# A three-layer graph attention kernel: partly filled gather columns packed densely, moved by one-hot products

## The chip, the cores and the metric

The kernel runs on one core of a Trainium2 chip. Its time is the device time of one execution in microseconds (us), from the first to the last instruction. Five engines work side by side, each on its own stream of instructions: PE (matrix products; PEld loads its weights), DVE (vector work), ACT (scalar work, exponentials and scaled copies), POOL (here mostly the issuer of indirect DMAs, which gather rows by index) and SP (the issuer of plain DMAs). "Span" is the profiler's first to last instruction.

## What is computed

There are 6250 nodes with 256 features and 100000 edges sorted by their target. Two GATv2 layers (4 heads of 64) with a self loop, a residual and a layer norm are followed by one GAT layer (8 heads of 32), a residual and a layer norm.

```python
def _gatv2_layer(x, src, dst, n, Wl, Wr, att, b):
    xl = (x @ Wl).reshape(n, H, C)
    xr = (x @ Wr).reshape(n, H, C)
    e = jax.nn.leaky_relu(xl[src] + xr[dst], NEG_SLOPE)
    logits = jnp.einsum('ehc,hc->eh', e, att)
    m = jax.ops.segment_max(logits, dst, num_segments=n)
    ex = jnp.exp(logits - m[dst])
    denom = jax.ops.segment_sum(ex, dst, num_segments=n)
    alpha = ex / (denom[dst] + 1e-16)
    msg = xl[src] * alpha[:, :, None]
    out = jax.ops.segment_sum(msg, dst, num_segments=n)
    return out.reshape(n, H * C) + b
...
h = _gatv2_layer(x, src, dst, n, Wl1, Wr1, att1, b1)
h = jax.nn.elu(h)
h = _gatv2_layer(h, src, dst, n, Wl2, Wr2, att2, b2)
...
x = _layernorm(x + _L0_gnn_ref(...), axis=-1)
x = _layernorm(x + _L1_gnn_ref(x, W, a, src, dst), axis=-1)
```

The third layer's logits are `leaky_relu(s1[src] + s2[dst])`, with one number for each node and head, and its messages are rows `Wh[src]`.

## The kernel before

**Blocks and columns.** `make_plan` sorts the nodes by their number of incoming edges, the largest first, and cuts them into 49 blocks of 128 nodes, one node in each partition. A block's edges become columns: column j of block b holds, for each of its 128 nodes, the row of that node's j-th source, or a row "nobody" (number NP) with a logit of -1.5e38 where the node has fewer. `columns` computes from the edge count alone, with bounds of 3.5 standard deviations, how many columns each block needs: 27 in block 0 (the few edges beyond are moved by one-hot products, `find_few`, `few_logits`, `few_sum`), then 25, 24, 23, 22, 21, ... down to 9 in block 48, 803 in all. One column is one indirect DMA on POOL (`gather_rows`, L1438).

**Packs.** The last column of some blocks is needed by a part of the nodes only. Before, ten such columns share three gathers ("packs": blocks 3, 13, 17, 36; blocks 26, 40, 47, 48; blocks 31, 43), with fixed row counts. `pick_rows` copies their indices together by SP's DMAs, `gather_pack` gathers them, `lay_rows` copies each part into its column, and `lack_rows` fills the column's other partitions with "nobody". The plan checks that no node needs more (`most`, L996).

**Buffers.** `rows` holds nine tiles of up to nine columns; a block of layer 1 or 2 takes three (two from block 18 on, where columns and self row are 18 or fewer). A tile is free again when PE has added its columns up, or in layer 3 when DVE has weighted them.

**The order, written out by hand.** Every engine runs its instructions in the order of the code. In `layer2`, which serves layers 1 and 2, the main loop does for block b:

1. `attend(b)`: on DVE, logits by three passes over each chunk (L1797, L1800, L1801; the first chunk's first pass, `first_z`, L1777, was already done in the block before), then the maximum (L1579); on ACT the exponentials (L1587), in layer 1 a copy of source numbers into `spots`; then the table rows of block b-2 are copied and written by SP (L1917), and `first_z(b+1)`.
2. `finish(b-1)` on ACT, then `weighted_sum(b)`: DVE multiplies rows by weights (L1633), ACT does it for the last `few` columns (L1629, four heads each), PE adds all columns up (L1640).
3. `fetch(b+2)` issues the lists of block b+4 (L1887), the pack work and `gather(b+2)`; then `turns` transposes on PE (L1558) and makes the next tables.

In layer 2 `fetch(b+2)` moves ahead, into `attend(b)`, where the buffers allow. `find_few` runs before `gather(0)`, `turns(0)`, `fetch(1)` and `turns(1)` in layer 1. `sort_sources` orders the first three blocks' sources, so that the following layer can gather their first 14, 12 and 11 columns (`EARLY`) before the last four blocks' rows are written: `begin`, called after the last `gather` of a layer, with the table cut at the rows of the first 45 blocks. In layer 3 the loop is `gather(b+1)`, `attend(b)` (L2010), weighting and adding on DVE (L1662, L1674), and a scatter of the finished rows on POOL (L2040).

**The plan's end.** `make_plan` writes the list of each node to DRAM (`near_d`, L1237) in two halves. Between them stand seven gathers into `spare` (L1254), a tile that nothing reads.

The two lines that the change's last part touches:

```python
few = min(S // 3, cut[-1][1] - cut[-1][0] - 1) if i == 0 else (2 * S - 2) // 3
few = few if b + 1 < NB else 0
```

Of the kernel before, what the change touches and what calls it, by code (L numbers as in the profile page):

```python
# [47 lines left out]
def columns(E, N, NB):  # L48
# [30 lines left out]
    part = {}  # L79
    for b in range(len(EARLY), NB):  # L80
        c = cols[b] - 1
        n = max(8, -(-int(math.ceil(over[c] + 3.5 * sd[c] - P * b)) // 8) * 8)
        if n < P:
            part[b] = n
    packs, taken = [], set()
    for b in sorted(part):
        if b in taken or part[b] > P * 3 // 4:
            continue
        pack, at = [], 0
        for k in range(b, NB):  # L90
            if k in part and k not in taken and at + part[k] <= P:
                pack.append((k, at, part[k]))
                at += part[k]
        if len(pack) > 1:
            packs.append(pack)
            taken.update(k for k, _, _ in pack)
    return cols, low, high, held, packs
# [569 lines left out]
def kernel(  # L667
# [22 lines left out]
    cols, low, high, held, packs = columns(E, N, NB)  # L690
# [7 lines left out]
    node_i = plan.tile([P, NB], I32, name="node_i")  # L698
    fits = plan.tile([P, 1], I32, name="fits")
# [11 lines left out]
    with tc.manual_schedule():  # L711
        make_plan(
            tc, x, src, dst, ((wl1, wr1, att1), (wl2, wr2, att2)), (b1, b2), w3, a3,
            cols, low, high, held, packs, node_i, fits, ident, eps, nobody, att, wc, wh, fixed, xl1_d,
            near_d,
        )
        nc.vector.memset(done, 0)
# [4 lines left out]
    with tc.If(ok != 0):  # L722
        with tc.manual_schedule():
            tile_by_degree(
                tc, x, att1, b1, b2, w3, a3, out, [held] + cols[1:], packs, node_i, near_d, ident, eps, nobody,
                xl1_d, att, wc, wh, fixed, done,
            )
# [8 lines left out]
def make_plan(  # L736
    ctx, tc, x, src, dst, layers, biases, w3, a3, cols, low, high, held, packs, node_i, fits, ident, eps,
    nobody, att, wc, wh, fixed, xl1_d, near_d,
# [36 lines left out]
    SPARE = 7  # L775
# [218 lines left out]
    for pack in packs:  # L994
        for b, _, n in pack:
            nc.gpsimd.tensor_scalar(  # L996
                most[:, b : b + 1], part_of, float(n), float(cols[b] - 1), op0=OP.is_lt, op1=OP.add
            )
# [252 lines left out]
    spare = one.tile([P, SPARE, LONG], I32, name="spare")  # L1251
    left(1, nc.gpsimd)
    for k in range(SPARE):
        nc.gpsimd.indirect_dma_start(  # L1254
            out=spare[:, k, :], out_offset=None, in_=listed,
            in_offset=bass.IndirectOffsetOnAxis(ap=begin_i[:, k : k + 1], axis=1),
        )
# [12 lines left out]
    counts = one.tile([P, NB], F32, name="counts")  # L1270
# [26 lines left out]
def tile_by_degree(  # L1297
    ctx, tc, x, att1, b1, b2, w3, a3, out, cols, packs, node_i, near_d, ident, eps, nobody,
    xl1_d, att, wc, wh, fixed, done,
# [52 lines left out]
    late = consts.tile([P, len(EARLY)], F32, name="late")  # L1352
# [41 lines left out]
    packed = {b: (q, r, n) for q, pack in enumerate(packs) for b, r, n in pack}  # L1394
    opens = {pack[0][0]: q for q, pack in enumerate(packs)}
    shuts = {pack[-1][0]: q for q, pack in enumerate(packs)}
    picks = [consts.tile([P, len(packs)], I32, name=f"pick{k}") for k in range(2)]
    for pick in picks:
        nc.gpsimd.memset(pick, NP)
    held_rows = {}  # L1400

    def pick_rows(q, pick, of):

        for b, r, n in packs[q]:
            nc.sync.dma_start(pick[r : r + n, q : q + 1], of[:n, b, cols[b] - 1 : cols[b]])

    def gather_pack(b, pool, name, pick, table, width):
        q = opens[b]
        held_rows[q] = pool.tile([P, RW], F32, name=name)
        nc.gpsimd.indirect_dma_start(  # L1410
            out=held_rows[q][:, :width], out_offset=None, in_=table,
            in_offset=bass.IndirectOffsetOnAxis(ap=pick[:, q : q + 1], axis=0),
        )

    def lay_rows(b, rows, width):

        q, r, n = packed[b]
        nc.sync.dma_start(rows[-1][:n, rows_at[b], :width], held_rows[q][r : r + n, :width])

    rows_at = {}  # L1420

    def lack_rows(b, rows, cut, table, width):

        n = packed[b][2]
        rows_at[b] = cut[-1][1] - cut[-1][0] - 1
        nc.sync.dma_start(
            rows[-1][n:, rows_at[b], :width],
            bass.AP(tensor=table.tensor, offset=table.offset + NP * width, ap=[[0, P - n], [1, width]]),
        )

    def gather_rows(b, rows, cut, own, table, of, width, j0, j1):


        for g, (s0, s1) in zip(rows, cut):
            for j in range(max(s0 - own, j0), min(s1 - own, j1)):
                if j + 1 == cols[b] and b in packed:
                    continue
# [88 lines left out]
    def sort_sources(work, ps, b):  # L1526

        n = cols[b]
# [19 lines left out]
        if b + 1 == len(EARLY):  # L1548
            pb = ps.tile([P, b + 1], F32, name="pb", tag="tp")
# [148 lines left out]
    def layer2(i, table, of, width, start, own, finish, follow):  # L1698
# [5 lines left out]
        with ExitStack() as es:  # L1704
# [5 lines left out]
            packp = es.enter_context(tc.tile_pool(name=f"pack{i}", bufs=len(packs)))  # L1710
# [5 lines left out]
            def gather(b):  # L1716
                first = EARLY[b] if b in begun else 0
                rows, cut = begun.pop(b) if first else row_tiles(b, 1)
                if b in opens:
                    gather_pack(b, packp, "pack", picks[i], table, width)  # L1720
# [119 lines left out]
            if i == 0:  # L1840
                find_few(work, pst)
# [274 lines left out]
```

## Time and profile before

| what | value |
|---|---|
| median of 14 runs | 3236.54 us (3235.97 to 3238.51) |
| profiled execution | 3237.21 us |
| its span | 3235.4 us |
| POOL | 2412.9 us busy (75%), 2587 instructions |
| DVE | 2714.9 us busy (84%), 2609 instructions |
| PE | 1399.1 us busy (43%) |
| ACT | 1281.8 us busy (40%) |
| DMA | 397.64 MB, 123 GB/s |

From the issue times of POOL, the first row gather of layer 1 starts at 104.2 us; the early gathers of layer 2 at 1159.55 and the rest of its block 0 at 1206.2; those of layer 3 at 2157.95 and 2204.2; the last gather at 3215.6. DMA-issuing instructions of POOL count as busy here, those of SP don't. "Idle before" in a group is the time the engine stood still just ahead of it; "issue" means that nothing the profile shows was waited for.

### The profile page before, as it was taken

To read this page: it belongs to the slowest core of one execution; us is meant where nothing else is said; L and a number is where in the kernel's file an instruction comes from. 1 tells how busy PE (TensorE), PEld (TensorE's weight loads), DVE (VectorE), ACT (ScalarE), POOL (GpSimd) and SP (SyncE) were. 2 spreads that over 40 slices of the span, in tenths; PEclk is the share of its full clock that TensorE was granted. 3 is DMA by queue.
4 is the path that set the end of the run, shared out by engine and by line. 5 is a ranking of instruction groups with operands and counts; after the bars stand their busy time and mean duration, and the time that the engine had idled before them with its cause. 6 is when DMAs were issued, how large, how long until landed. Compare 5 with 4: busy or idle time off the path is not lost.

```text
span 3235.4 us, 25460 instructions
## 1 busy us (share of the span) xinstructions
PE 1399.1 (43%) x5424; PEld 1122.3 (35%) x5424; DVE 2714.9 (84%) x2609; ACT 1281.8 (40%) x5161; POOL 2412.9 (75%) x2587
## 2 busy tenths in 40 slices
PE   8266656666677754666566566770000000000000
PEld 6255545554565643545445455550000000000000
DVE  8599999898899978999989999994966767666677
ACT  3234444444445535777667777770000000000001
POOL 5677777777777777777777777777777777777776
PEclk9677887878888986887877888885555555555555
DMA  9544444444444454444444444544334433434343
GB/s 259 125 113 125 119 118 123 118 122 124 124 123 127 125 147 112 124 122 129 128 123 127 130 133 133 136 128 113 109 107 109 110 108 107 109 109 110 109 110 95
DMA packets 176463, 397.64 MB, mean 123 GB/s; under 512 B 50923, under 2 KB 93955, under 8 KB 176283
## 3 DMA queue, kind: packets, MB, share of 16 engines
q0 software_dynamic: 120608, 336.86, 39.8%
q1 hardware_dynamic: 53992, 57.08, 5.9%
q10 hardware_dynamic: 1700, 1.97, 0.3%
q8 instruction: 48, 0.79, 0.1%
q14 instruction: 115, 0.94, 0.1%
HBM read 354.60 MB, written 40.42 MB: 122 GB/s over the span
## 4 chain that ended last, share of the span: by engine, by line
POOL 25%; DVE 17%; issue 14%; DMA 5%; PE 4%; ACT 1%; DVEq 0%; POOLq 0%; SPq 0%; ACTq 0%
POOL g L1438 24%; DVE z L1800 3%; DVE lg L1801 3%; PE acc L1640 3%; DMA g<-xl_d,near_r 2%; DVE z L1797 2%; DVE z L1777 2%; DVE g L1633 2%; DMA g<-whs_d,near_r 2%; DVE weighted L1662 1%; POOL out L2040 1%; DMA out<-y,node_i 1%; DVE acc_v L1674 0%; DVE stats L1684 0%; ACT g L1629 0%
## 5 line engine op out<-in xcount | busy, mean ns | idle before, releaser
L1438 POOL DMA_INDIRECT g<-xl_d,near_r x1549 | 1465.7, 946 | 473.8 <-issue 419.1
L1640 PE MATMUL acc<-g,ident 128*128 128x256 f32 x3408 | 966.8, 452 | 631.0 <-DVE g L1633 316.6
L1640 PEld LDWEIGHTS acc<-g,ident 128*128 128x128 f32 x3408 | 777.5, 232 | 821.2 <-DVE g L1633 334.6
L1438 POOL DMA_INDIRECT g<-whs_d,near_r x756 | 717.7, 949 | 230.3 <-issue 220.2
L1629 ACT ACTIVATE g<-g,by 128x64 f32<-128x64 f32 x3080 | 744.9, 336 | 28.3 <-DVE by L1596 28.0
L1801 DVE TENSOR_REDUCE lg<-z 128x28 f32<-128x1820 f32 (+4 forms) x234 | 497.4, 2125 | 8.1
L1800 DVE TENSOR_TENSOR z<-z,at 128x1820 f32<-128x1820 f32 (+4 forms) x234 | 496.8, 2123 | 4.7
L1797 DVE TENSOR_TENSOR z<-g,pr 128x1820 f32<-128x1820 f32 (+3 forms) x138 | 299.7, 2172 | 44.5 <-DMA g<-xl_d,near_r 34.6
L1604 ACT ACTIVATE wt<-lg 128x128 f32<-128x128 f32 (+17 forms) x49 | 14.0, 285 | 799.8 <-DVE lg L1603 799.8
L1674 DVE TENSOR_REDUCE acc_v<-weighted 128x256 f32<-128x3584 f32 (+10 forms) x47 | 319.0, 6787 | 1.6
L1633 DVE TENSOR_TENSOR g<-g,at 128x256 f32<-128x256 f32 (+8 forms) x185 | 273.6, 1496 | 3.3
L1587 ACT ACTIVATE at<-lg,top 128x19 f32<-128x19 f32 (+14 forms) x392 | 115.3, 294 | 379.6 <-DVE top L1579 362.9
L1777 DVE TENSOR_TENSOR z<-g,pr 128x2080 f32<-128x2080 f32 (+4 forms) x96 | 197.9, 2062 | 72.5 <-DMA g<-xl_d,near_r 31.0
L2010 DVE TENSOR_TENSOR lg<-g,s_r 128x56 f32<-128x56 f32 (+4 forms) x111 | 23.0, 215 | 253.7 <-DMA g<-whs_d,near_r 232.2
L1662 DVE TENSOR_TENSOR weighted<-g,wt 128x1792 f32<-128x1792 f32 (+4 forms) x111 | 227.1, 2058 | 0.3
L1563 ACT COPY xT<-pt 128x256 f32<-128x256 f32 x147 | 50.2, 374 | 402.0 <-PE pt L1558 402.0
L1568 PE MATMUL pm<-wcat,xT 128*128 128x260 f32 x392 | 94.2, 383 | 1.4 <-ACT xT L1563 1.4
L1568 PEld LDWEIGHTS pm<-wcat,xT 128*128 128x128 f32 x392 | 74.2, 190 | 13.4 <-ACT xT L1563 2.1
L1587 ACT ACTIVATION_READ_ACCUMULATOR at<-lg,top 128x1 f32 x392 | 73.2, 187 | 0.0
L1568 PE MATMUL pm<-wh_cat,xT 128*128 128x272 f32 x196 | 58.0, 419 | 22.6 <-ACT xT L1563 22.6
L2040 POOL DMA_INDIRECT out<-y,node_i x49 | 49.8, 1017 | 23.0 <-issue 14.2
L1688 ACT ACTIVATE sd<-mv,eps 128x1 f32<-128x1 f32 x98 | 29.0, 296 | 93.0 <-DVE mv L1686 93.0
(267 smaller groups left out, 1592.6 us busy)
## 6 DMA issues: line engine op xcount, KB each, us to landing
g<-xl_d,near_r POOLq DMA_INDIRECT x1549, 2.8
g<-whs_d,near_r POOLq DMA_INDIRECT x756, 2.8
whs_d<-row SPq DMA_DIRECT2D x49, 132.0 KB
xl_d<-row SPq DMA_DIRECT2D x49, 130.0 KB
xr_d<-row SPq DMA_DIRECT2D x49, 130.0 KB
two<-xl_d SPq DMA_DIRECT2D x49, 130.0 KB
two<-xr_d SPq DMA_DIRECT2D x49, 130.0 KB
near_d<-x_all SPq DMA_DIRECT2D x7, 896.0 KB
```

Of the source, the lines that this page charges most:

```text
L1438: nc.gpsimd.indirect_dma_start(out=g[:, j + own - s0, :width], out_offset=None, in_=table, in_offset=source(of, b, j),)
L1568: nc.tensor.matmul(pm, xT[:, c, :], w[:, c, :], start=c == 0, stop=c == 1)
L1587: nc.scalar.activation(wt[:, :, h], lg[:, :S, h], AF.Exp, bias=top[:, h : h + 1], accum_out=den[:, h : h + 1],)
L1629: nc.scalar.mul(g4[:, t, h, :], g4[:, t, h, :], by[:, s0 + t - a0, h : h + 1])
L1633: nc.vector.tensor_mul(g4[:, :m], g4[:, :m], wt[:, s0 : s0 + m, :].unsqueeze(3).to_broadcast([P, m, H, F // H]),)
L1640: nc.tensor.matmul(acc, ident, g4[:, t], start=False, stop=s0 + t == S - 1 and not more)
L1662: nc.vector.tensor_mul(prod[:, s0 - base : s1 - base, :].rearrange("p t (h d) -> p t h d", h=H), g[:, :n, :F].rearrange("p t (h d) -> p t ...
L1674: nc.vector.reduce_sum(part, prod[:, : s1 - base, :].rearrange("p s f -> p f s"), axis=AX.X)
L1777: nc.vector.tensor_max(z, rows[0][:, :n, :W2], xr[:, None, :].to_broadcast([P, n, W2]))
L1797: nc.vector.tensor_max(z, g[:, :n, :W2], xr[:, None, :].to_broadcast([P, n, W2]))
L1800: nc.vector.tensor_mul(z, z, at[:, None, :].to_broadcast([P, n, W2]))
L1801: nc.vector.reduce_sum(lg[:, s0:s1, :], z.rearrange("p t (h d) -> p t h d", h=H2), axis=AX.X)
```

## The change

`columns` no longer builds packs. A new `lanes_of` lists every column of blocks 1 to 48 whose number of real rows may be under three quarters of a block: 33 items. `base[b]` is the number of columns still gathered one by one (770 in all with block 0's 27). The real rows of all items are put one after the other in a dense list of 14 x 128 rows, which 14 gathers per layer fetch. Where an item starts in the list is only known at run time, so:

- `find_lanes` (layer 1, after `find_few`) counts each item's rows with a product on PE and a running sum on DVE, and keeps the starts in `lane_i` for SP and in `lane_in` for the picks. `shut` is a penalty of -1.5e38 for partitions without a row.
- `pick_lanes` moves the source numbers into the dense list: two DVE operations (a one-hot by row and the source numbers placed by pack) and one PE product per item, one add and a cast per call. It is called before `gather(0)` for the items of blocks 1 and 2, in `attend(0)` for those up to block 20, and then in `fetch(b)` whenever lists beyond were loaded.
- `gather` in layer 1 loads the lists (`begins`) as far ahead as the next packs need: for block 1 up to block 20.
- `gather_packs` gathers the packs that fall due (0, 1 and 2 at block 2, then one at blocks 4, 6, 8, 9, 16, 20, 21, 26, 35, 45 and 47); `keep_packs` writes each to DRAM (SP); `lay_rows` reads each item's rows back from DRAM at an offset that SP loads into a register; `pick_again` reads back the numbers that layers 2 and 3 need.
- `lack_rows` fills what an item can't reach, `shut_lanes` adds the penalty to the logits of the items' columns.
- the seven `spare` gathers and the ten masks of `most` are gone.
- in layer 1 ScalarE's share of the weighting goes from a third to two fifths of the columns, with the same cap, the last chunk less one.

The core of the diff:

```diff
...
+def lanes_of(N, NB, mean, pmf, over, sd, cols, low, high):
...
+    items, top, base = [], [], list(cols)
+    assert cols[1] <= high
+    for b in range(1, NB):
+        size = min(P, N - P * b)
+        for c in range(low, cols[b]):
+            if min(size, over[c] - 3.5 * sd[c] - P * b) < 0.75 * P:
+                base[b] = min(base[b], c)
+                items.append((b, c))
+                top.append(max(8, min(P, -(-math.ceil(over[c] + 3.5 * sd[c] - P * b) // 8) * 8)))
...
-    spare = one.tile([P, SPARE, LONG], I32, name="spare")
     left(1, nc.gpsimd)
-    for k in range(SPARE):
-        nc.gpsimd.indirect_dma_start(
-            out=spare[:, k, :], out_offset=None, in_=listed,
-            in_offset=bass.IndirectOffsetOnAxis(ap=begin_i[:, k : k + 1], axis=1),
...
+    items, top, base, lo, hi, need, filled_by = lanes
+    base[0] = cols[0]
+    K = len(need)
+    upon = [max(2, b) for b in need]
...
+        for b, own in items_of.items():
+            nc.vector.tensor_scalar(
+                has[:, own[0] : own[-1] + 1], numbers[:, base[b] : cols[b]], counts[:, b : b + 1],
+                None, op0=OP.is_lt,
+            )
+        pn = ps.tile([P, len(items)], F32, name="lane_n", tag="tp")
+        nc.tensor.matmul(pn, ones, has, start=True, stop=True)
+        nc.vector.tensor_scalar(shut, has, -1.0, BIG, op0=OP.add, op1=OP.mult)
...
+        nc.vector.tensor_tensor_scan(
+            at, ones[:, : len(items) + 1], n, 0.0, op0=OP.mult, op1=OP.add
+        )
+        nc.vector.tensor_max(held_at, at, bound[:, 0])
+        nc.vector.tensor_tensor(held_at, held_at, bound[:, 1], op=OP.min)
+        nc.vector.tensor_copy(lane_i, held_at[:1, : len(items)])
...
+    def lane(i):
+        _, (v,) = nc.values_load_multi_w_load_instructions(
+            lane_i[:, i : i + 1], engines=[mybir.EngineType.SP], min_val=lo[i], max_val=hi[i],
+            skip_runtime_bounds_check_because="the lane was brought within these bounds",
+        )
+        nc.sync.nop()
+        return bass.ds(v, top[i])
+    def pick_lanes(work, ps, lists):
+        first = written[0]
+        while written[0] < len(items) and items[written[0]][0] < lists:
+            written[0] += 1
+        if written[0] == first:
+            return
+        pk = ps.tile([P, K], F32, name="lane_k", tag="tp")
+        for i in range(first, written[0]):
+            b, c = items[i]
+            own = items_of[b]
+            if i == own[0]:
+                nc.vector.tensor_single_scalar(
+                    lane_in[:, 2, i : own[-1] + 1], sources[:, b, base[b] : cols[b]], -float(NP),
+                    op=OP.add,
+                )
+            hot_l = work.tile([P, P], F32, name="lane_hot", bufs=2)
+            nc.vector.tensor_scalar(hot_l, numbers, lane_in[:, 0, i : i + 1], None, op0=OP.is_equal)
+            given = work.tile([P, K], F32, name="lane_given", bufs=2)
+            nc.vector.tensor_scalar(
+                given, numbers[:, 1 : K + 1], lane_in[:, 1, i : i + 1], lane_in[:, 2, i : i + 1],
+                op0=OP.is_equal, op1=OP.mult,
+            )
+            nc.tensor.matmul(pk, hot_l, given, start=i == first, stop=i + 1 == written[0])
+        nc.vector.tensor_add(pick_f, pick_f, pk)
+        full = [q for q in range(K) if first <= filled_by[q] < written[0]]
+        if full:
+            nc.vector.tensor_copy(
+                picks[0][:, full[0] : full[-1] + 1], pick_f[:, full[0] : full[-1] + 1]
+            )
+    def gather_packs(b, pool, pick, table, width):
+        for q in packs_at.get(b, ()):
+            held_rows[q] = pool(q)
+            nc.gpsimd.indirect_dma_start(
+                out=held_rows[q][:, :width], out_offset=None, in_=table,
+                in_offset=bass.IndirectOffsetOnAxis(ap=pick[:, q : q + 1], axis=0),
+            )
+    def keep_packs(b, k):
+        for q in packs_at.get(b, ()):
+            nc.sync.dma_start(pack_d[k][q * P : (q + 1) * P, :], held_rows[q][:, : wide[k]])
+    def pick_again(b):
+        for q in packs_at.get(b, ()):
+            nc.sync.dma_start(
+                picked[:, q : q + 1], pack_d[0][q * P : (q + 1) * P, W2 : W2 + 1]
+            )
+    def lay_rows(b, rows, cut, own, k):
+        for i in items_of.get(b, ()):
+            j = items[i][1] + own
+            g, s0 = next((g, s0) for g, (s0, s1) in zip(rows, cut) if s0 <= j < s1)
+            nc.sync.dma_start(g[: top[i], j - s0, : wide[k]], pack_d[k][lane(i), :])
...
+    def shut_lanes(b, lg, own, H):
+        if b in items_of:
+            i0, n = items_of[b][0], len(items_of[b])
+            s = lg[:, base[b] + own : cols[b] + own, :]
+            nc.vector.tensor_add(s, s, shut[:, i0 : i0 + n].unsqueeze(2).to_broadcast([P, n, H]))
...
+                if i == 0 and b:
+                    begun_lists[0] = min(NB, 1 + max(
+                        [b + 2] + [items[filled_by[q]][0] for q in range(K) if upon[q] <= b + 2]
+                    ))
+                    for k in range(begun_lists[0]):
+                        begins(k)
+                gather_rows(b, rows, cut, 1, table, of, width, first, base[b])
+                lack_rows(b, rows, cut, 1, table, width)
+                if b == 1:
+                    waiting.append(lambda: lay_rows(b, rows, cut, 1, i))
+                else:
+                    lay_rows(b, rows, cut, 1, i)
+                    if i == 0:
...
-                if i == 0 and b + 2 in opens:
-                    for k, _, _ in packs[opens[b + 2]]:
-                        begins(k)
-                if i == 0 and b + 1 in opens:
-                    pick_rows(opens[b + 1], picks[0], sources)
+                if i == 0 and b > 1:
+                    pick_lanes(work, pst, begun_lists[0])
+                gather_packs(b, pack_tile, picks[i], table, width)
+                keep_packs(b, i)
...
+                shut_lanes(b, lg, 1, H2)
+                if i == 0 and b == 0:
+                    pick_lanes(work, pst, begun_lists[0])
-                few = min(S // 3, cut[-1][1] - cut[-1][0] - 1) if i == 0 else (2 * S - 2) // 3
+                few = min(2 * S // 5, cut[-1][1] - cut[-1][0] - 1) if i == 0 else (2 * S - 2) // 3
...
                 find_few(work, pst)
+                find_lanes(zp, pst)
+                pick_lanes(work, pst, 3)
             gather(0)
...
```

## The prediction

> **What bounds it now.** I read the page's busy shares first: DVE 84%, POOL 75%, neither full. The table of stages corrects that picture. Its columns are the window, its length, and busy time with instruction count for PE, PEld, DVE, ACT and POOL.
>
> ```profile
> 200.00:400.00 200.00, 129.01 (x520) 106.53 (x518) 190.86 (x174) 80.31 (x330) 151.26 (x161) 0.82 0.47 120
> 690.00:1190.00 500.00, 357.85 (x1424) 291.15 (x1422) 456.04 (x414) 242.61 (x993) 378.27 (x400) 0.87 0.49 127
> 1500.00:1800.00 300.00, 182.57 (x658) 144.19 (x658) 271.13 (x221) 210.53 (x869) 226.90 (x241) 0.79 0.47 127
> 2204.00:3220.00 1016.00, 2.65 (x6) 1.51 (x6) 724.96 (x775) 66.66 (x193) 770.22 (x810) 0.50 0.40 109
> ```
>
> POOL issues 0.80 instructions per us in every stage, so one per 1.25 us: it never stops. DVE is at 90 to 95% in layers 1 and 2 (to about 2200 us) and at 71% in layer 3. So POOL bounds layer 3 alone, and layers 1 and 2 together with a DVE that has almost no room. The waits say the same:
>
> ```profile
> L1438 POOL DMA_INDIRECT g<-xl_d,near_r x1549 | 1465.7, 946 | 473.8 <-issue 419.1
> ...
> POOL g L1438 <- issue: 657.9, 2160, 0.3
> POOL g L1438 <- PE acc L1640: 27.5, 84, 2.2
> DVE z L1777 <- DMA g<-xl_d,near_r: 31.0, 17, 6.3
> ```
>
> A gather is 0.946 us plus a 0.30 us gap; the one real stall of POOL between 104 and 3220 us is 2.2 us at 1246.8. Third, the timeline where one block of layer 1 gives way to the next (block 3; start, duration, what):
>
> ```profile
> 260.25 2.61 DVE L1633 TENSOR_TENSOR g<-g,at 128x2048 f32<-128x2048 f32 x2
> 262.77 2.04 DVE L1800 TENSOR_TENSOR z<-z,at 128x1820 f32<-128x1820 f32 x1
> ...
> 260.04 13.69 PE L1640 MATMUL acc<-g,ident 128*128 128x256 f32 x48 [2.31 <-DVE row L1884]
> 273.56 0.38 PE L1558 MATMUL pt<-ident,near_r 128*128 128x128 f32 x2
> ```
>
> DVE leaves the weighting at 262.86 and starts the next block's logits at once. PE still adds that block up until 273.56, and serves nothing queued behind until then.
>
> **Fewer gathers (gain).** From the plan's column counts, a layer issues 803 columns - 10 packed + 3 packs + 1 = 797 gathers before, and 770 + 14 + 1 = 785 after: 12 x 1.25 = 15.0 us of POOL per layer. In layer 3 POOL is the bound and DVE is idle 24 to 34 us of each 100, so 15.0 is gained, less about 1.3 at the end: there DVE finishes block 47 before it can take block 48, and of the last block's two gathers (2.5 us) only the wait from 3217.7 to 3219.3 goes. Layer 3: **-13.7**.
>
> **The plan.** The 7 spare gathers (74.97 to 84.8 us) go, but POOL then waits 3.14 us for DVE's list at 87.9 anyway: 0. The ten masks of `most` lie ahead of a 16.6 us wait: 0. Without that cover they would be worth 9 and 3 us.
>
> **Start of layer 1 (loss).** The first picks need the lists of blocks 3 to 20, so 18 list gathers go ahead of block 1's rows where 4 stood. POOL, from its issue times:
>
> ```profile
> 138.08 0.95 POOL L1474 DMA_INDIRECT few_row<-xl_d,few_at  x1 [0.30 <-issue]
> 144.33 0.95 POOL L1438 DMA_INDIRECT g<-xl_d,near_r  x1 [0.30 <-issue]
> ...
> 178.32 2.59 DVE L1797 TENSOR_TENSOR z<-g,pr 128x2340 f32<-128x2340 f32 x1
> ```
>
> Block 1's rows start at 139.33 + 18 x 1.25 = 161.8; 23 of them end at 190.6; packs 0 to 2 follow, the last issued at 193.1. Only then can block 1's last two columns be laid: pack landing 3.7 (its median), write to DRAM 2.5 (as `out`'s rows), two register loads and issues on SP at about 1.3 each (the SP load of `done` took 0.61, a lay's issue 0.6), read back 2.75 (the load of `two`): 204.7. DVE took that chunk at 178.3: **+26.4**. DVE's own new work there is in its shadow: `find_lanes`, about 85 small memsets x 0.1, 27 compares x 0.2 and 16 others = 18 us; 14 picks, 14 us; part of this fell in idle time, and the chunk would be +21 late by that alone. So bounds +21 to +32.
>
> The Trainium skill (DMA: Bandwidth & Descriptors, "Anatomy of one DMA") puts a fixed 2.0 us, mostly write receipt, on each transfer plus bytes over 436 GB/s. By it, estimated, write and read of 133 KB are 2.3 us each instead of 2.5 and 2.75, and the chunk is ready 0.7 us sooner. No run here isolates it.
>
> **Later picks (loss, the largest).** After block 0, `pick_lanes` runs inside `fetch`, behind `weighted_sum(b)`. Its matmuls queue on PE behind that block's acc matmuls, and its `tensor_add(pick_f, pick_f, pk)` waits for them on DVE; behind that add stand the next block's logits, and everything after. The trace has no such wait; nearest are the transposes, which stand at that very place in PE's queue, and this return trip on an empty PE:
>
> ```profile
> 106.02 0.16 DVE L1454 COPY few_got<-few_o 128x1 f32<-128x1 f32 x1 [0.80 <-PE few_o L1453]
> ```
>
> By the bounds of the lists, nine calls carry items (19 in all), after blocks 1, 3, 5, 6, 13, 17, 18, 23 and 32. From DVE's end of weighting to the start of the transposes is 10.9, 10.7, 9.9, 9.2, 8.4, 7.4, 8.5, 7.6, 8.2: sum 80.8. Each adds 0.8 + 0.45 (a second item's matmuls), the add 0.2 and the cast 0.25: 9 x 1.7 = 15. **+95**, the one-hots (0.28 + 0.23 an item) lying within. Low end: PE costs nothing and only DVE's instructions count, 9 x 2.6 = 23; high end 105. I take 95, since both engines take this code in order.
>
> **Small DVE edits.** `shut_lanes`: 27 adds of 0.2 (as the add of 128x44 at L1491): +5.4 per layer. ScalarE's two fifths is capped by the last chunk less one; it changes nothing up to block 17 and moves one column in 28 blocks. A column is 2.06 - 1.75 = 0.3 us of DVE: **-8**; ACT gets 28 x 4 x 0.24 = 27 us while under 50% busy: 0. If ACT's later end held PE up, that would be 0 instead of -8.
>
> The Trainium skill (SBUF — State Buffer, "Who interferes with whom") speaks against these one-hots: a one-source DVE operation in a two-port mode shuts GpSimd out for its whole length. The gather beside the compare at 106.29 took 1.05 us instead of 0.95. By the rule 33 x 0.28 = 9 us of POOL, by the row 3; either lies in layer 1, where POOL will wait anyway.
>
> **DVE's slack.** With DVE this late its waits for rows vanish. Idle ahead of L1777 and L1797 between 187.6 and 1190 us is 5.4 + 19.8 + 26.5 = 51.7; I count **-50** (bounds 40 to 52).
>
> **Sum.** End of layer 1, DVE: 26.4 + 95 + 5.4 - 8 - 50 = +68.8. Layer 2's first gathers need the rows of block 44, written at 1154.0 and landed about 1156.5; POOL came at 1159.55. So layer 2 starts 3.1 less late: +65.7. In layer 2 POOL is only 3 or 4 gathers ahead by blocks 12 to 25, where DVE waits 22.6 us for rows, and 12 ahead at the end, where it waits 12.3; layer 3 needs both and starts at about 65.7 - 15.0 = +50.7 (DVE agrees: 65.7 + 5.4 of `shut_lanes` - 15 of waits = 56, less the 5 by which its rows landed before POOL came). The two new round trips to DRAM at block 1 of layers 2 and 3 end some 2 us before DVE comes; uncovered, 3 us each. Layer 3: 50.7 - 13.7 = **+37**. The profiled execution took 3237.2 us (span 3235.4 and 1.8 around it), 0.7 above the median of the runs: 3274 in both terms.
>
> **Rivals.** *A, the picks are cheap* (0.12): PE answers within DVE's other work. Then 95 becomes 23, DVE ends layer 1 at -3, layer 2 starts at -6, layer 3 at -19, the end is -33: 3204. For it: PE is 43% busy. Against: the order of the code and 273.56 above. It decides once a call costs DVE under 5.5 us: the nine then cost 50, 45 less than forecast, and the rest of the 37 is within layer 2's slack. *B, SP's queue is the new wait* (0.11, slower): `keep_packs` holds SP until a pack lands, then up to three register loads and lays stand ahead of the table rows. Every last chunk then comes late; at 1 us in each of 27 blocks of layer 2 and at the last rows of both layers, +20 to +35: about 3300. Against: SP's longest waits are for ACT's rows, up to 44.9 us, so it is idle when asked. *C, POOL decides alone* (0.03): 43 x 1.25 = 54 less, 3183. Against: DVE's 95%.
>
> **Chances.** My forecast 0.74, A 0.12, B 0.11, C 0.03. Its own range is 3245 to 3300, from the bounds of start, calls and slack. To hold 8 in 10 the range reaches 3240 to 3306. About 0.2% (6.5 us) is what runs of this kernel can tell from no change. Faster 0.15 (A and C), same 0.05 (the forecast's low edge), slower 0.80.
>
> **What would show it.** Nine DVE waits of 9 to 12 us at the new `tensor_add` on PE; block 1's last chunk in layer 1 at about 205 us; POOL waiting for PE acc in layer 1; layer 2's first gather near 1225 instead of 1159.6; layer 3 shorter by 14 us. I am wrong if those waits are under 6 us, or if POOL stays back to back through layer 1.

## The result and the profile after

The changed kernel takes 3281.35 us (median of 6 runs, 3277.55 to 3282.63), the kernel before 3236.80 us beside it (28 runs): 1.0135 times as long, 95% interval 1.0126 to 1.0145, or 44.6 us more. The forecast of 3274 was 7 us low and the time lies in its range. The profiled execution has a span of 3277.8 us against 3235.4, 42.4 more.

The first view is the table of waits after (who waited, for whom, us in total, times, longest):

```profile
POOL g L1568 <- issue: 644.7, 2092, 3.8
DVE pick_f L1508 <- PE lane_k L1507: 71.6, 11, 9.5
POOL g L1568 <- PE acc L1770: 47.2, 64, 21.8
POOL two L1523 <- DVE pick L1511: 41.6, 6, 11.6
DVE z L1918 <- DMA g<-xl_d,near_r: 13.2, 5, 6.7
```

The second row is new: the add of `pick_lanes` stands still on VectorE for TensorE. The fourth is what follows from it on GpSimd: a pack's gather can't be issued before its index is there. The third was 27.5 us before, with a longest wait of 2.2; now one wait is 21.8. The last was 31.0.

The timeline of one such call (after, fetch of block 7; start, duration, what, in brackets the idle time before):

```profile
390.33 12.67 PE L1770 MATMUL acc<-g,ident 128*128 128x256 f32 x44 [18.27 <-DVE row L2029]
402.85 0.51 PE L1507 MATMUL lane_k<-lane_given,lane_hot 128*128 128x14 f32 x4
...
392.81 0.15 DVE L1496 TENSOR_SCALAR lane_in<-near_r 128x1 f32<-128x1 int32 x1
403.40 0.17 DVE L1508 TENSOR_TENSOR pick_f<-pick_f,lane_k 128x14 f32<-128x14 f32 x1 [9.37 <-PE lane_k L1507]
403.60 0.15 DVE L1511 CAST pick<-pick_f 128x1 int32<-128x1 f32 x1
403.67 2.04 DVE L1941 TENSOR_TENSOR z<-z,at 128x1820 f32<-128x1820 f32 x1
...
401.82 0.94 POOL L1568 DMA_INDIRECT g<-xl_d,near_r  x1 [0.30 <-issue]
404.02 0.94 POOL L1523 DMA_INDIRECT two<-xl_d,pick  x1 [1.26 <-DVE pick L1511]
```

VectorE had made its one-hot tiles by 394.03. TensorE is at the acc matmuls until 402.85 and takes the product only then; the product itself is 0.5 us long. The next block's logits (L1941) stand behind the add on VectorE, and the next pack's gather behind the cast on GpSimd.

How full VectorE and GpSimd are in layer 1, before and after (stage, length, busy time and count of PE, PEld, DVE, ACT, POOL, then clock, DMA share, GB/s). Before:

```profile
500.00:700.00 200.00, 128.32 (x496) 104.71 (x495) 181.09 (x151) 91.67 (x377) 151.43 (x160) 0.79 0.46 121
700.00:900.00 200.00, 138.40 (x534) 112.85 (x533) 177.24 (x139) 86.09 (x349) 151.21 (x160) 0.82 0.47 122
```

After:

```profile
500.00:700.00 200.00, 125.37 (x494) 102.48 (x493) 178.86 (x169) 83.40 (x346) 140.34 (x150) 0.77 0.44 115
700.00:900.00 200.00, 136.37 (x537) 111.45 (x536) 179.72 (x157) 98.59 (x405) 138.87 (x147) 0.81 0.43 115
```

GpSimd's 160 instructions in 200 us were its full pace; now it issues 150 and 147. VectorE's busy time hardly moves, and its waits for picks come on top: it is the one that is full.

GpSimd at the border of layers 1 and 2, after (`soon` is the index tile of layer 2's early gathers; before, the first of them stood at 1159.55, straight behind the last of layer 1):

```profile
1196.84 0.95 POOL L1568 DMA_INDIRECT g<-xl_d,near_r  x1 [0.31 <-issue]
1219.56 0.94 POOL L1568 DMA_INDIRECT g<-xl_d,soon  x1 [21.78 <-PE acc L1770]
```

So the loss is 60.0 us by the end of layer 1. Layer 2 gives 13.5 back (its last stretch begins 46.5 later: 2204.50 against 2157.95 for the first early gather of layer 3), layer 3 another 14.5 (the last row gather goes out 32.1 later). At the end 3.9 us are lost up to the last scatter (3265.19 against 3229.25): VectorE takes block 47's last chunk 36.0 us later than before (3243.12 against 3207.11) and goes on from there to the end at its old pace. 6.4 more are lost behind the last scatter. 60.0 - 13.5 - 14.5 + 3.9 + 6.4 = 42.3, where the spans differ by 42.4.

The last term is in the queue of GpSimd, in a DRAIN at the end of the program and an instruction INC_SWDGE_SEM just ahead of it. Before (duration in ns, shortest, median, longest, then first and last start):

```profile
L2112 POOLq DRAIN  x3: 46/107/1137, 3233.4 to 3235.1; - x3
...
L729 POOLq INC_SWDGE_SEM  x1: 460/460/460, 3232.9 to 3232.9; - x1
```

After:

```profile
L2265 POOLq DRAIN  x3: 50/107/6275, 3270.6 to 3277.5; - x3
...
L754 POOLq INC_SWDGE_SEM  x1: 1715/1715/1715, 3268.9 to 3268.9; - x1
```

The longest DRAIN takes 5.14 us more and INC_SWDGE_SEM 1.26, at the same point of the program.

### The profile page after: what moved, and what is told of

It reads as the page before. It is cut to its first block, busy times and chain, and to the rows that moved or that the text cites. A ratio compares the mean times of both kernels' runs of the same rounds, so it can differ in the third digit from the quotient of the medians.

```text
span 3277.8 us, 26731 instructions
## 1 busy us (share of the span) xinstructions
PE 1413.5 (43%) x5492; PEld 1133.3 (35%) x5492; DVE 2748.2 (84%) x2938; ACT 1307.7 (40%) x5274; POOL 2369.6 (72%) x2532
## 4 chain that ended last, share of the span: by engine, by line
POOL 25%; DVE 15%; issue 14%; DMA 7%; PE 2%; ACT 1%; DVEq 0%; POOLq 0%; ACTq 0%
POOL g L1568 24%; DVE z L1941 4%; DVE lg L1942 3%; DMA g<-xl_d,near_r 3%; DMA g<-whs_d,near_r 2%; DVE z L1938 2%; DVE z L1918 2%; PE acc L1770 2%; DVE g L1763 2%; POOL out L2193 1%; DMA out<-y,node_i 1%; ACT g L1759 1%; ACT at L1717 0%; DVE stats L1814 0%; PE pm L1698 0%
## 5 line engine op out<-in xcount | busy, mean ns | idle before, releaser
L1568 POOL DMA_INDIRECT g<-xl_d,near_r x1503 | 1422.4, 946 | 472.3 <-issue 411.9
L1568 POOL DMA_INDIRECT g<-whs_d,near_r x733 | 696.1, 950 | 223.3 <-issue 209.6
L1759 ACT ACTIVATE g<-g,by 128x64 f32<-128x64 f32 x3192 | 771.4, 336 | 6.6 <-DVE by L1726 6.6
L1941 DVE TENSOR_TENSOR z<-z,at 128x1820 f32<-128x1820 f32 (+4 forms) x234 | 496.8, 2123 | 4.7
L1763 DVE TENSOR_TENSOR g<-g,at 128x256 f32<-128x256 f32 (+7 forms) x185 | 266.2, 1456 | 3.3
```

Of the source, the lines that this page charges most:

```text
L1568: nc.gpsimd.indirect_dma_start(out=g[:, j + own - s0, :width], out_offset=None, in_=table, in_offset=source(of, b, j),)
L1759: nc.scalar.mul(g4[:, t, h, :], g4[:, t, h, :], by[:, s0 + t - a0, h : h + 1])
L1763: nc.vector.tensor_mul(g4[:, :m], g4[:, :m], wt[:, s0 : s0 + m, :].unsqueeze(3).to_broadcast([P, m, H, F // H]),)
L1941: nc.vector.tensor_mul(z, z, at[:, None, :].to_broadcast([P, n, W2]))
```

## The experiments

Each was compared with runs of the kernel before on the same chip (medians 3234.2 to 3234.9 us); differences below are against those. On that scale the change itself is +44.6.

**Undo the wait, keep the rest.** The calls of `pick_lanes` move from `fetch` to `attend`, where TensorE has nothing long in its queue.

```diff
 def fetch(b):
-    if i == 0 and b > 1:
-        pick_lanes(work, pst, begun_lists[0])
 def attend(b):
-    if i == 0 and b == 0:
-        pick_lanes(work, pst, begun_lists[0])
     wt, new = weights(work, ps1, lg, n, H2, wt, few, S)
...
     while behind:
         behind.pop()()
+    if i == 0:
+        pick_lanes(work, pst, begun_lists[0])
```

> The calls of pick_lanes stand in attend, behind the weights of a block and ahead of its weighted sum, instead of in fetch. Theory (the one-hot products wait behind the block's acc matmuls on PE): each of the nine later waits of pick_f on lane_k falls from about 8.5 us to about 1, so VectorE gets about 74 us back in layer 1; the first gathers of layer 2, at 1219.6 in the changed kernel, are then set by GpSimd's own pace, 1159.6 + 23.9 (later start) - 15 (fewer gathers) = about 1168, plus some data waits: 1168 to 1185. Total about 3237 us (3228 to 3250). Rival (the loss is VectorE's added instructions and the later start, the waits only stand in for data waits): 3265 or more, with the data waits of first_z and of its copy back at their 72 and 44 us.

3225.36 us, 9.1 less than before (ratio 0.9971, 0.9959 to 0.9983), 53.7 better than the change as made. From its table of waits:

```profile
DVE pick_f L1508 <- PE lane_k L1507: 22.0, 11, 3.1
```

and GpSimd's timeline at its border of layers 1 and 2:

```profile
1143.43 0.95 POOL L1568 DMA_INDIRECT g<-xl_d,near_r  x1 [0.30 <-issue]
1166.18 0.95 POOL L1568 DMA_INDIRECT g<-xl_d,soon  x1 [21.80 <-DVE g L1763]
```

The add waits 22.0 us instead of 71.6, the nine calls behind block 0 take 35.7 us of VectorE instead of 89.3, GpSimd waits for no pick any more (the row `two` on `pick` is gone), and layer 2 begins 53.4 us sooner than in the changed kernel, at 1166.18, where 1168 to 1185 was expected. The total came out 3 us under the lower edge of the range I gave. Nothing else was altered, so the place of the calls is worth 53.7 us, more than the whole loss: placed here, the change is a gain. GpSimd had issued all of layer 1 by 1144.4, 15 us sooner than before, and then waited: VectorE still ends this layer.

**The wait alone.** The kernel before, with one product and one add at the nine places; nothing reads the sum.

```diff
 def fetch(b):
...
+    if i == 0 and b in (3, 5, 7, 8, 15, 19, 20, 25, 34):
+        pk = pst.tile([P, 14], F32, name="probe_k", tag="tp")
+        nc.tensor.matmul(pk, ident, numbers[:, :14], start=True, stop=True)
+        nc.vector.tensor_add(probe, probe, pk)
```

> The kernel before with nothing of the change but one 128x128 by 128x14 product on PE and one VectorE add of its result at the nine places in fetch where the changed kernel calls pick_lanes. Theory: each add waits 8 to 9.5 us for PE behind the acc matmuls, 9 x 9 = 81 us of VectorE's time in layer 1, of which its data waits there give back about 50: total 3236.8 + 25 to 40 = about 3270 us. Rival (a PE answer is quick, and the nine waits of the changed kernel come from the lists or the gathers that its products need): 0 to 5 us more.

3272.52 us, +38.1 (ratio 1.0118, 1.0102 to 1.0133). The row of the wait:

```profile
DVE probe L1747 <- PE probe_k L1746: 83.9, 9, 10.8
```

Nine adds of 0.17 us wait 83.9 us and cost 38.1. VectorE's own idle time gave the other 46 back, nearly all of it ahead of the first passes over the rows, where the idle time of layer 1 falls from 51.7 us to 8.0. The lists and picks that such a product needs in the changed kernel have no part in it.

**Whose wait is it?** In the changed kernel GpSimd waits for picks too (41.6 us). Picking one block earlier should take GpSimd's wait away and leave VectorE's.

```diff
-    [b + 2] + [items[filled_by[q]][0] for q in range(K) if upon[q] <= b + 2]
+    [b + 2] + [items[filled_by[q]][0] for q in range(K) if upon[q] <= b + 2 + (b > 1)]
```

> The changed kernel with seven of its nine later calls of pick_lanes, and the lists that they need, one block earlier; the calls stay in fetch, behind the acc matmuls. GpSimd's wait of two on pick (41.6 us in the changed kernel) should fall to about 5, VectorE's wait of pick_f on lane_k should stay near 70. Theory of the prediction (the price is VectorE's time): nearly all of the loss stays, 3268 to 3282 us. Rival (the price is GpSimd's, which stands still until the pick is there, and VectorE has room): 41.6 less, about 3240 us.

3282.07 us, +47.6 (ratio 1.0146, 1.0131 to 1.0162): no gain.

```profile
DVE pick_f L1508 <- PE lane_k L1507: 70.2, 11, 10.1
...
POOL two L1523 <- DVE pick L1511: 16.3, 2, 14.1
```

GpSimd's wait for picks fell by 25 us (one of 14.1 remained, so not to the 5 expected) and the time did not follow. 41.6 us of idle GpSimd in the table of waits were a shadow of VectorE's, not a price.

**The later start alone.** The kernel before, with the lists of blocks 4 to 20 ahead of block 1's rows.

```diff
+    if i == 0 and b == 1:
+        for k in range(21):
+            begins(k)
     gather_rows(b, rows, cut, 1, table, of, width, first, cols[b])
```

> The kernel before with the lists of blocks 4 to 20 gathered ahead of block 1's rows, as the changed kernel has them, and nothing else. Prediction's term: the start of layer 1 moves by about 17 x 1.25 = 21 us for VectorE and is carried to the end of the layer, 3234 to 3237 + 15 to 21 = about 3255 us. Rival (GpSimd issues as many gathers as before and never waits in layer 1, and VectorE's data waits of some 98 us there take the shift up): 0 to 5 us more.

3234.57 us, unchanged (ratio 1.0000, 0.9990 to 1.0009). Block 1 does come late:

```profile
172.54 2.32 DVE L1780 TENSOR_TENSOR z<-g,pr 128x2080 f32<-128x2080 f32 x1 [23.76 <-DMA g<-xl_d,near_r]
```

VectorE stands 23.76 us there (before, it took this chunk at 154.72, after a wait of 4.80), and layer 2 begins at 1157.98, no later than before. GpSimd issues the same gathers in another order, and VectorE makes the shift good out of its later idle time: from 200 to 1100 us it is busy for 851.0 us, against 833.6 before.

**Both together.** The nine waits and the early lists in the kernel before:

```diff
+    if i == 0 and b == 1:
+        for k in range(21):
+            begins(k)
...
+    if i == 0 and b in (3, 5, 7, 8, 15, 19, 20, 25, 34):
+        pk = pst.tile([P, 14], F32, name="probe_k", tag="tp")
+        nc.tensor.matmul(pk, ident, numbers[:, :14], start=True, stop=True)
+        nc.vector.tensor_add(probe, probe, pk)
```

> The kernel before with both the nine waits of e4_before_nine_waits (3272.5 alone) and the early lists of e8_before_lists_first (no change alone). If the later start is carried to the end once VectorE has no room left, as the prediction's sum has it: 3272.5 + 15 to 21 = about 3290 us. Rival (GpSimd's reordering is absorbed in any case): 3272 to 3276 us, so that the rest of the changed kernel's loss would be VectorE's added instructions.

3288.93 us, +54.1 (ratio 1.0166, 1.0150 to 1.0181): 16.0 more than the nine waits alone. The same shift that costs nothing by itself costs three quarters of its 21 us once the waits have used VectorE's room up. Layer 2 begins at 1157.98 with the lists alone, 1195.63 with the waits alone and 1211.80 with both: the two bring 53.8 of the 60.0 us that the changed kernel loses by that point.

**The share of ScalarE, three ways.** The changed kernel with one third again:

```diff
-    few = min(2 * S // 5, cut[-1][1] - cut[-1][0] - 1) if i == 0 else (2 * S - 2) // 3
+    few = min(S // 3, cut[-1][1] - cut[-1][0] - 1) if i == 0 else (2 * S - 2) // 3
```

> The changed kernel with ScalarE weighting one third of a block's columns again (S // 3 in place of 2 * S // 5). Prediction's term: 8 us of VectorE's time in layer 1 come back on the path, 3281 + 8 = about 3289 us (3285 to 3292). Rival (the share is hidden, VectorE's own data waits take it up): 3281 within 2.

3286.92 us, +52.4 (ratio 1.0161, 1.0146 to 1.0177), 7.8 above the change's +44.6 (5.6 between the two medians, which come from different chips). Layer 2 begins at 1227.98 against 1219.56, 8.4 us later.

`e1_picks_in_attend` with a half:

```diff
-    few = min(2 * S // 5, cut[-1][1] - cut[-1][0] - 1) if i == 0 else (2 * S - 2) // 3
+    few = min(S // 2, cut[-1][1] - cut[-1][0] - 1) if i == 0 else (2 * S - 2) // 3
```

> e1_picks_in_attend with ScalarE weighting half of a block's columns in layer 1 (S // 2 in place of 2 * S // 5). In e1 GpSimd has issued its last row gather of layer 1 at 1143.4 and then waits 21.8 us for VectorE to end the layer: if VectorE sets the end of layer 1 there, relief of VectorE moves the first gathers of layer 2 ahead by about as much as the step from a third to two fifths did in the changed kernel (5.6 us): 3225.4 - 5 = about 3220 us, the wait of g at the boundary falling to about 16. Rival (ScalarE, ahead of the last products on PE, now sets the end of a block): 3225 or more.

3217.48 us, -17.4 (ratio 0.9944, 0.9929 to 0.9959), 8.3 better than e1, and the fastest kernel of this study. Its border of the layers:

```profile
1159.68 0.94 POOL L1568 DMA_INDIRECT g<-xl_d,soon  x1 [18.00 <-DVE row L2027]
```

GpSimd still waits 18.0 us for VectorE there, so VectorE still ends the layer.

The kernel before with a half:

```diff
-    few = min(S // 3, cut[-1][1] - cut[-1][0] - 1) if i == 0 else (2 * S - 2) // 3
+    few = min(S // 2, cut[-1][1] - cut[-1][0] - 1) if i == 0 else (2 * S - 2) // 3
```

> The kernel before with ScalarE weighting half of a block's columns in layer 1 (S // 2 in place of S // 3), nothing else: the same relief of VectorE, in full, that gave 5.6 us from a third to two fifths in the changed kernel and 7.9 us from two fifths to a half in e9_picks_and_half. If GpSimd's own pace sets the end of layer 1 before, as e8_before_lists_first says: 3235 within 2 us, the first gathers of layer 2 still near 1159. Rival (VectorE sets it there too, and the share is a gain by itself): 13 us less, about 3222 us, and e9's lead over before would be the share's alone.

3234.61 us, unchanged (ratio 1.0000, 0.9990 to 1.0010), layer 2 at 1157.99. What is worth 8 us in the changed kernel, and 8 more in e1, is worth nothing before, where GpSimd's pace ends layer 1. e9's lead is not the share's alone.

**The drain.** The seven spare gathers put back into the changed kernel, and taken out of the kernel before:

```diff
+    spare = one.tile([P, SPARE, LONG], I32, name="spare")
     left(1, nc.gpsimd)
+    for k in range(SPARE):
+        nc.gpsimd.indirect_dma_start(
+            out=spare[:, k, :], out_offset=None, in_=listed,
+            in_offset=bass.IndirectOffsetOnAxis(ap=begin_i[:, k : k + 1], axis=1),
+        )
```

> The seven spare gathers of the plan are put back into the changed kernel, all else as changed. Theory (the DRAIN of GpSimd's queue at the end of the program, 1.14 us before and 6.28 us after, depends on how many indirect gathers went before, and with it INC_SWDGE_SEM 0.46 against 1.72): DRAIN near 1.1, INC_SWDGE_SEM near 0.5, total 3275 us. Rival (the DRAIN has to do with something else that the change does): DRAIN stays at 6.3 and the total at 3281 (the plan's end does not move, as something else ends it) or above, up to 3288 if the seven gathers at 0.95 us are on the plan's path.

Put back: 3280.26 us, +45.8 (ratio 1.0140, 1.0125 to 1.0156): no gain, and a longer DRAIN.

```profile
L2272 POOLq DRAIN  x3: 50/107/6847, 3272.2 to 3279.6; - x3
...
L754 POOLq INC_SWDGE_SEM  x1: 1855/1855/1855, 3270.3 to 3270.3; - x1
```

> The kernel before without its seven spare gathers, nothing else. Theory (the count of indirect gathers sets the final DRAIN): DRAIN goes from 1.1 to somewhere up to 6.3 us and the total from 3236.8 to up to 3243. Rival (the spares are just dead work beside the plan): 3236.8 unchanged, or up to 6.6 us less if they are on the plan's path.

Taken out of the kernel before: 3244.63 us, +10.2 (ratio 1.0031, 1.0019 to 1.0042).

```profile
L2105 POOLq DRAIN  x3: 46/107/9222, 3233.0 to 3242.8; - x3
...
L729 POOLq INC_SWDGE_SEM  x1: 2435/2435/2435, 3230.6 to 3230.6; - x1
```

All of it, 8.1 + 2.0, is in these two rows; the last scatter goes out no later (3227.13 against 3229.25). My first idea (fewer gathers, longer drain) was too simple: seven more made it longer in one kernel and seven fewer in the other. Counting every indirect DMA of the program gives an order: 2470 after, 2477 with the spares back, 2506 here, 2513 before, with DRAINs of 6.28, 6.85, 9.22 and 1.14 us. It rises by 0.082 us for each, and falls back somewhere between 2506 and 2513. So e1 with 43 gathers that nobody reads, 2513 in all (the `spares` of `begin2` and of the end read rows of `xl_d`, by `node_i`):

```diff
+    def spares(k0, k1):
+        for k in range(k0, k1):
+            nc.gpsimd.indirect_dma_start(
+                out=spare[:, k, :], out_offset=None, in_=listed,
+                in_offset=bass.IndirectOffsetOnAxis(ap=begin_i[:, k % SEGS : k % SEGS + 1], axis=1),
+            )
+    spares(0, 9)
     key = one.tile([P, NB], BF16, name="key_b")
...
     left(1, nc.gpsimd)
+    spares(9, 18)
...
         if k0 >= HALF_S * STEP:
             filled(k0, k1)
+    spares(18, 23)
...
     def begin2():
+        spares(0, 17)
         begin(1, xl2_d, W2)
...
         for b in sorted(puts):
+            if b + 1 == NB:
+                spares(17, 20)
             put_out(*puts[b], apart=True)
```

> The calls of pick_lanes in attend as in e1_picks_in_attend, and 43 indirect gathers that nobody reads in places where GpSimd is idle: 23 in the plan, 17 ahead of the first gathers of layer 2, 3 ahead of the last scatter. Theory (the DRAIN at the end grows by 0.082 us and INC_SWDGE_SEM by 0.020 us with each indirect gather, and starts again every 106: 1.14 us before, 9.22 with 7 fewer, 6.28 with 43 fewer, 6.85 with 36 fewer): DRAIN 1.1, INC_SWDGE_SEM 0.46, 6.4 us less than 3225.4, about 3219 us. Rival (position in the program or kind of gather counts, not their number): DRAIN above 6 and 3225 us or more.

3226.42 us, -8.1 (ratio 0.9975, 0.9965 to 0.9984).

```profile
L2288 POOLq DRAIN  x3: 50/107/1130, 3224.5 to 3226.2; - x3
...
L754 POOLq INC_SWDGE_SEM  x1: 460/460/460, 3224.0 to 3224.0; - x1
```

The drain is that of the kernel before to within 10 ns, though this is the changed code, and the time is not better than e1's: layer 1 begins 5.7 us later (first list gather at 104.93 against 99.21), and GpSimd's first instruction there waits for the landing of the last spares:

```profile
103.94 0.24 POOL L1360 IOTA numbers<- 128x128 f32 x1 [5.24 <-DMA spare<-list_d,begin_i]
```

The last scatter goes out at 3218.35 against 3211.24. With those five moved behind the last row gathers:

```diff
-    spares(18, 23)
...
         for b in sorted(puts):
-            if b + 1 == NB:
-                spares(17, 20)
+            spares(*((17, 19) if b + 1 < NB else (19, 25)))
             put_out(*puts[b], apart=True)
```

> As e6_picks_and_43_spares, but the five spare gathers at the end of the plan, whose landing the first instructions of layer 1 waited for (5.7 us later than in e1), stand in GpSimd's idle time behind the last row gathers, 2 ahead of the last scatter but one and 6 ahead of the last. Theory: DRAIN stays at 1.1 and the start of layer 1 goes back to within 1.5 us of e1's 99.2: 3225.4 - 6.4 + 1 to 2 = about 3220.5 us. Rival (the spares beside the plan and at the boundary cost as much as the DRAIN gives): 3224 or more.

3227.06 us, -7.8 (ratio 0.9975, 0.9964 to 0.9985). The start came back by 2.0 us only (102.93), so the landing of those five was the smaller part of the 5.7; the last scatter goes out at 3215.51, 4.3 later than e1's. What the count of gathers gives at the end, these places take. A place that costs nothing was not found.

## Why the prediction was right, and where it was off

The main step held: picks ordered behind a block's weighted sum wait for its acc matmuls on TensorE, and VectorE pays. The nine calls of the changed kernel take 89.3 us of VectorE, from first instruction to the next block's work (77.0 of it waiting), where the sum had 95. The waits are 7.3 to 9.5 us long, three of them over 9, where 9 to 12 was forecast; in the ninth call, of three items, VectorE waits at the one-hot tile (6.84) and not at the add (0.48). The wait's removal (e1) and the wait alone (e4) show it from both sides. The Trainium skill (PSUM — Partial Sum Buffer, "Engine vs sequencer instructions") states the rule behind it, that matmuls start and complete in program order; the timeline agrees: the product starts at 402.85, as the block's acc matmuls end (403.00 by their modelled end).

Term by term, to the end of layer 1:

| term | predicted | measured |
|---|---|---|
| block 1's last chunk, start of layer 1 | +26.4 | +23.7 (201.99 against 178.32) |
| nine calls | +95 | +89.3 |
| `shut_lanes` | +5.4 | +4.4 (27 adds) |
| two fifths | -8 | -7.8 (one third against it) |
| VectorE's waits for rows, gone | -50 | -44 (51.7 before, 7.9 left beside block 1's) |
| sum | +68.8 | +65.6 |

The first row rests on this line of the changed kernel:

```profile
201.99 2.59 DVE L1938 TENSOR_TENSOR z<-g,pr 128x2340 f32<-128x2340 f32 x1 [6.92 <-DMA near_r<-near_d,node_i]
```

The profile puts this wait down to a list; in e5 and e9 it puts the same wait (8.6 and 7.8 us) down to `g<-pack_d`, the read-back of the packs, as the prediction had it. The 2.0 us that the prediction cites for one transfer stand in a section on DMAs that GpSimd issues, while this write and read are SP's, and no run splits their times; its 0.7 us stays open. In the fifth row the profile names the rows' DMAs for 21.9 of the 51.7 us and ScalarE for 29.3; what went is VectorE's idle time, whoever ended it.

VectorE ended layer 1 62.4 us later than before (its last weighting at 1246.9 against 1184.5); 3 us of the measured terms' sum are not assigned. That the two sums lie so close is in part luck: the forecast put 2.7 us too much on the start, 5.7 on the calls and 1.0 on `shut_lanes`, and took 6 too much off for the waits. Layer 2's first gathers came 60.0 later (65.7 predicted), layer 3's 46.5 (50.7).

Three things were off. **The terms are not additive**, as the sum treated them. The start (+26.4) and the share (-8) are right only beside the nine waits: alone in the kernel before, both are worth nothing (e8, and e12 with a half), beside the waits 16 of 21 and 7.8. The -50 of slack was in effect spent on the first comer. That this gave the right total is because the waits were large enough to use all the slack. **Rival A's sum was too low by 21**: e1 is the kernel that it described, and takes 3225 instead of 3204. 13 us of that lie at the end of layer 1, which it put 6 us earlier than before and which came 6.6 later: the nine calls, put at 23 us of VectorE, still take 35.7 in e1; 6.4 are the drain, 2.6 the tail. **The end of the program was missed**: 3.9 us were lost up to the last scatter where 1.3 was put, and 6.4 us of DRAIN and INC_SWDGE_SEM that the step "The plan" excluded. It costed the removed spare gathers, as dead work beside a wait, at nothing. The work was dead; the number of gathers was not. Without the drain, the median would have come to 3275, 1 us from the forecast.

Rival B did not come: SP waits long for packs (up to 130.4 us in layer 3; the 44.9 that the prediction gives for before is the longest of the row with the largest total, and its longest single wait was 206.6), but layers 2 and 3 were as much shorter as fewer gathers make them (13.5 and 14.5 of 15.0), which late last chunks would not allow. Rival C is out: the 24 gathers fewer of layers 2 and 3 are worth 28 us, the 12 of layer 1 nothing while VectorE ends it, and the 7 of the plan less than nothing.

## What to carry to other kernels

An answer that one engine needs from another costs what stands ahead of it in the other's queue, not what it takes: here 0.5 us of TensorE became 7.3 to 9.5, nine times. Ask for such a product where the answering queue is empty, even if the code reads better elsewhere; moving one call turned +1.35% into -0.3%, and with more of VectorE's work on ScalarE -0.6%. When two engines are both nearly full, measure each term in the kernel it will stand in: the early lists cost 0 or 16 us, ScalarE's share gave 0 or 8, by which engine ended the layer.

## What the hardware showed unasked

In these runs GpSimd's last DRAIN grows with the number of indirect DMAs issued before it, 0.082 us each, and INC_SWDGE_SEM by 0.020, until both fall back (to 1.14 and 0.46 at 2513). Three of the four counts tried lie on one line and the fourth beyond the fall; where exactly it falls back, and after how many gathers again, was not measured, and the rows that the DMAs move were not varied apart from their number. Extended downwards, the line reaches the value of 2513 near 2407, so a period of about 106 is an estimate.

Beside a gather, it was mostly the one-hot compares that waited, not GpSimd, and only beside a part of it. After, in block 0's picks:

```profile
155.46 0.41 DVE L1501 TENSOR_SCALAR lane_hot<-numbers,lane_in 128x128 f32<-128x128 f32 x1
155.92 0.28 DVE L1501 TENSOR_SCALAR lane_hot<-numbers,lane_in 128x128 f32<-128x128 f32 x1
156.65 0.48 DVE L1501 TENSOR_SCALAR lane_hot<-numbers,lane_in 128x128 f32<-128x128 f32 x1 [0.20 <-PE lane_k L1507]
...
162.78 0.28 DVE L1501 TENSOR_SCALAR lane_hot<-numbers,lane_in 128x128 f32<-128x128 f32 x1
...
154.88 0.95 POOL L2032 DMA_INDIRECT near_r<-near_d,node_i  x1 [0.30 <-issue]
156.13 0.95 POOL L2032 DMA_INDIRECT near_r<-near_d,node_i  x1 [0.30 <-issue]
...
162.38 0.95 POOL L1568 DMA_INDIRECT g<-xl_d,near_r  x1 [0.30 <-issue]
```

The compare at 155.92 begins behind the first gather's end and takes 0.28 us. Of the 33 compares of the changed kernel, the ten that begin 0.47 to 0.65 us into a gather all end 0.05 us behind that gather's end (155.87 against 155.83, 157.13 against 157.08) and take 0.35 to 0.53. The six that begin in its first 0.40 us, as the one at 162.78 does, run through inside it in 0.28. Of seven gathers that begin while a compare runs, five keep their 0.95 us and two take 0.97 and 1.04. The Trainium skill (SBUF — State Buffer, "Who interferes with whom") says that whoever issues first holds the shared ports and the other blocks. The ten late compares fit that; the six early ones don't, as they run inside a gather that was there first, and why is open. The prediction put this at 9 us of GpSimd by the rule and 3 by its own row; in this trace VectorE pays 1.8 us in all, and GpSimd 0.1.
